# An AdaLN block on one core: loads and first norms in another order, keys kept in pairs of blocks, 640-column scores cut at 384

## The chip, the core and the metric

The kernel runs on one core of a Trainium2 chip. Times are device microseconds (us) of one execution. Three timed executions gave 2437.5, 2437.94 and 2440.83 us; the median, 2437.94 us, is the time before. The profile is of another execution, which took 2422.97 us. The engines are TensorE (PE, with its weight loads as PEld), VectorE (DVE), ScalarE (ACT), GpSimd (POOL) and SyncE (SP), which here only issues transfers.

## What is computed

All data is float32. One token block of 2048 rows and 512 columns goes through an attention layer and a mixture-of-experts layer, each behind a layer norm that is scaled and shifted by a modulation row. Cut to what the change touches, the reference is:

```python
mod = (_silu(L0_c) @ L0_wmod).reshape(1, 6, 1, -1)      # six rows of 512
sa, ca, ga, sb, cb, gb = (mod[:, i] for i in range(6))
h = _layernorm(x, axis=-1) * (1 + ca) + sa
q = jnp.einsum('bpm,hmd->bphd', h, Q_w) + Q_b           # 16 heads of 128; k and v alike
logits = jnp.einsum('bqhd,bkhd->bhqk', q, k) / math.sqrt(128)
scores = softmax(where(key > query, NEG, logits))        # causal, over 2048 keys
attn = jnp.einsum('bhqk,bkhd->bqhd', scores, v)
x = x + ga * (jnp.einsum('bqhd,hdm->bqm', attn, O_w) + O_b)
# then a second norm with sb, cb, and 64 routed experts and 2 shared ones, scaled by gb
```

## The kernel before

The work runs in three stages: a prologue (up to 54.4 us in the profile), the attention over 16 heads (to 1667 us), and the output projection's rest with the experts (to the end). Only the first two are touched.

**Prologue.** SP issues the loads in the order of the code: `c` (L264), then for each of four blocks of 512 tokens the block `xb` of x (L269, 1 MB). After block 0 it issues the two modulation weights `wm` for rows 1 (`ca`) and 0 (`sa`) (L277, 1 MB each), after block 1 the weights of head 0 (L150, L151) and three biases (L286), and after block 3 the weights of the next heads. `mod_row(i)` (L309, L314) makes one modulation row on PE and copies it out with DVE; `mod_turn(i)` (L319, L327) turns it into columns `modT`. `norm_x(b)` (L333 to L339) takes the statistics of a block on DVE, a square root on ACT (L336), a reciprocal (L337), and normalises the block in place with four instructions (L339). `turn_x` (L351) transposes a half of the normalised block on PE into one of two PSUM tiles; `place_x` (L360, ACT) scales and shifts it by `modT` into `hT` and frees the PSUM tile. `plain` (L168, L175) makes the keys and queries of head 0. The order of the calls, written out in the code, is the order on every engine: each engine works through its own instructions in that order.

**Attention.** The work is cut into 80 steps, 5 for each head. Step s of a head handles one or two pairs of 128-row query tiles: pairs 7, 6, (5, 0), (4, 1), (3, 2). `softmax_tile` takes a query tile's causal width in chunks of up to 1024 keys. For each chunk, PE makes the scores in products of up to 512 columns (L500), DVE adds the causal mask on the last 128 columns (L512), takes the row maximum (L513, L517), and ACT makes the exponentials (L519), which frees the PSUM tile `ps`; there are two such tiles, of 1024 columns each. Widths are multiples of 128; a chunk of 640 columns is a product of 512 and one of 128. There are two such chunks in a head (query tiles 4 and 12), 32 in all. Blocks of the finished probabilities are swapped by DMA (L544), turned by DVE (L554), and multiplied with the values on PE (L572).

The scores run two steps ahead of the values. `merge` interleaves the scores, the value products and "fillers" by their share of columns done. The fillers of steps 0 to 2 make queries and keys of the next head: `project(hd + 1, 1)` for tokens 1024 to 2047, then `project(hd + 1, 0)` for tokens 0 to 1023, each of seven parts `first` to `seventh` with a product of their own (L217). The third part writes the keys of the lower block of 512 of its two with one DVE instruction (L235), the fourth those of the upper one (L243). Step 1 of head `hd` ends with the third part of `project(hd + 1, 0)`; in the same step, running two ahead, stand the scores of step 3 of head `hd`, among them the second chunk of query tile 8 (1152 keys: 1024 and 128).

**Keys.** `ktp` is a pool of six tiles of 512 keys each. A head uses four. A new tile is given when one is free, and a tile is free when its last reader is done. Of the keys 1024 to 2047 of a head, the upper tile (1536 to 2047) is read for the last time in step 1 of the head, the lower one (1024 to 1535) in step 3, by that 128-column product.

The lines that follow are the functions that the change touches, with the line numbers of the profile before.

Of the kernel before, what the change touches and what calls it, by code (L numbers as in the profile page):

```python
# [9 lines left out]
F32 = mybir.dt.float32  # L10
# [8 lines left out]
P = 128  # L19
# [4 lines left out]
def adaln_block_kernel(  # L24
# [23 lines left out]
    nc = tc.nc  # L48
    _, N, D = x.shape
    H, _, DH = Q_w.shape  # L50
    E, _, HE = Wg.shape
    S, _, HS = Sg.shape
# [3 lines left out]
    DC = D // P  # L56
# [4 lines left out]
    SC = 1024  # L61
# [59 lines left out]
    with ExitStack() as att:  # L121
        enter = att.enter_context
# [10 lines left out]
        qkb = acst.tile([P, 4, H], F32)  # L133

        qkw = enter(tc.tile_pool(name="qkw", bufs=1))
        ktp = enter(tc.tile_pool(name="ktp", bufs=6))
        qtp = enter(tc.tile_pool(name="qtp", bufs=6))
        heads = {}
        groups = {}
        kts = {}  # L140
        qts = {}
        vts = {}

        def load_head(hd):
            if hd == 0:
                wq, wk = [ktp.tile([P, DC, DH], F32, name="kt") for _ in range(2)]
            else:
                wq = qkw.tile([P, DC, DH], F32, name="wq")
                wk = qkw.tile([P, DC, DH], F32, name="wk")
            nc.sync.dma_start(out=wq, in_=Q_w[hd].rearrange("(k p) d -> p k d", p=P))  # L150
            nc.sync.dma_start(out=wk, in_=K_w[hd].rearrange("(k p) d -> p k d", p=P))  # L151
            return wq, wk
# [10 lines left out]
        def plain(b, j, dst):  # L163
# [12 lines left out]
                dst, ps, AF.Identity, bias=qkb[:, b, 0:1], scale=scale if b == 0 else 1.0  # L176
            )

        def first_tiles():
            for j in (2, 3, 0, 1):  # L180
                kts[0, j] = ktp.tile([P, 512], F32, name="kt")
            for j in (3, 2, 1, 0):
                qts[0, j] = qtp.tile([P, 512], F32, name="qt")

# [22 lines left out]
        def project(hd, b):  # L207


            i, j = 2 * b, 2 * b + 1  # L210
            T = Ts[b]
            box = {}

            def product(l, r):
                ps = psA.tile([P, 512], F32, name="pqk", tag="mm")
                for k in range(2):
                    nc.tensor.matmul(  # L217
                        out=ps, lhsT=l[:, k], rhs=r[:, k], start=(k == 0), stop=(k == 1)
                    )
                return ps  # L220

            def first():
                box["p"] = qkw.tile([P, 512], F32, name="p_")
                ps = product(heads[hd][0][:, 0:2, :], hTs[i][:, 0:2, :])
                nc.scalar.activation(
                    box["p"], ps, AF.Identity, bias=qkb[:, 0, hd : hd + 1], scale=1.0
                )

            def second():
                q = qts[hd, j] = qtp.tile([P, 512], F32, name="qt")  # L230
                nc.vector.tensor_add(q, box["p"], product(sums_w[hd][:, 1], T[:, 1]))

            def third():
                k = kts[hd, i] = ktp.tile([P, 512], F32, name="kt")
                nc.vector.scalar_tensor_tensor(  # L235
                    k, product(sums_w[hd][:, 2], T[:, 2]), qkb[:, 3, hd : hd + 1], qts[hd, j],
                    ALU.add, ALU.add,
                )

            def fourth():  # L240
                k = kts[hd, j] = ktp.tile([P, 512], F32, name="kt")
                ps = product(sums_w[hd][:, 0], T[:, 0])
                nc.vector.tensor_add(k, kts[hd, i], ps)  # L243
                nc.vector.tensor_add(qts[hd, j], qts[hd, j], ps)

            def fifth():
                k = kts[hd, i]
                nc.vector.tensor_sub(k, k, product(heads[hd][1][:, 2:4, :], T[:, 3]))

            def sixth():  # L250
                q = qts[hd, j]
                nc.vector.tensor_add(q, q, product(sums_w[hd][:, 3], hTs[j][:, 2:4, :]))

            def seventh():
                q = qts[hd, i] = qtp.tile([P, 512], F32, name="qt")
                nc.vector.tensor_add(
                    q, box["p"], product(heads[hd][0][:, 2:4, :], hTs[i][:, 2:4, :])
                )

            return [(1024, f) for f in (first, second, third, fourth, fifth, sixth, seventh)]  # L260

        with tc.tile_pool(name="pre", bufs=1) as pre, tc.manual_schedule():
            c4 = pre.tile([DC, P], F32)
            nc.sync.dma_start(out=c4, in_=c.rearrange("o (k p) -> (o k) p", p=P))  # L264
            xs = []
            b16s = []
            for b in range(NB):
                xb = pre.tile([P, 4, D], F32, name="xb", bufs=NB)
                nc.sync.dma_start(  # L269
                    out=xb, in_=x[0, b * 512 : (b + 1) * 512, :].rearrange("(i p) d -> p i d", p=P)  # L270
                )
                xs.append(xb)
                if b == 0:
                    wms = {}
                    for i in (1, 0):
                        wms[i] = pre.tile([P, DC, D], F32, name="wm", bufs=2)
                        nc.sync.dma_start(  # L277
                            out=wms[i],
                            in_=wmod[:, i * D : (i + 1) * D].rearrange("(k p) n -> p k n", p=P),
                        )  # L280
                if b == 1:
                    heads[0] = load_head(0)
                    first_tiles()
                    for src in (Q_b, K_b, V_b):
                        b16 = pre.tile([H, DH], F32, name="b16", bufs=3)
                        nc.sync.dma_start(out=b16, in_=src)  # L286
                        b16s.append(b16)
            groups[0] = load_group(0)
            heads[1] = load_head(1)
            groups[1] = load_group(1)  # L290
# [38 lines left out]
            def norm_x(b):  # L329
                mv = pre.tile([P, 4, 2], F32, name="mv", bufs=2)  # L330
                for i in range(4):
                    st = pre.tile([P, 6], F32, name="st", bufs=4)
                    nc.vector.bn_stats(st, xs[b][:, i, :])  # L333
                    nc.vector.bn_aggr(mv[:, i, :], st)
                rstd = pre.tile([P, 4], F32, name="rstd", bufs=2)
                nc.scalar.activation(rstd, mv[:, :, 1], AF.Sqrt, bias=eps, scale=1.0)  # L336
                nc.vector.reciprocal(rstd, rstd)  # L337
                for i in range(4):
                    nc.vector.tensor_scalar(  # L339
                        xs[b][:, i, :], xs[b][:, i, :], mv[:, i, 0:1], rstd[:, i : i + 1],  # L340
                        ALU.subtract, ALU.mult,
                    )

            turns = {}

            def turn_x(b, half):
                tp = psA.tile([P, 2, 512], F32, name="tp", tag="sc")
                for j in range(2):
                    k = 2 * half + j
                    for i in range(4):  # L350
                        nc.tensor.transpose(  # L351
                            tp[:, j, i * P : (i + 1) * P], xs[b][:, i, k * P : (k + 1) * P], ident
                        )
                turns[b, half] = tp
# [7 lines left out]
                        scale=mod[1][:, k : k + 1], bias=mod[0][:, k : k + 1],  # L362
                    )

            norm_x(0)
            mod_row(1)
            turn_x(0, 0)
            mod_turn(1)
            mod_row(0)
            turn_x(0, 1)  # L370
            mod_turn(0)
            place_x(0, 0)
            place_x(0, 1)
            norm_x(1)
            bps = psA.tile([P, 3, H], F32, name="bps", tag="po")
            for b in range(3):
                nc.tensor.transpose(bps[:, b], b16s[b], ident[:H, :H])
# [5 lines left out]
            for b in range(1, NB):  # L383
                for half in range(2):
                    turn_x(b, half)
                    place_x(b, half)
                if b + 1 < NB:
                    norm_x(b + 1)
                if b == 2:
                    sum_h(0)  # L390
                plain(1, b - 1, kts[0, b - 1])
# [17 lines left out]
        for g in range(1, NG):  # L409
            o = vplace[g - 1]  # L410
# [46 lines left out]
        def softmax_tile(hd, s, pr, i, pb):  # L457
# [35 lines left out]
            def chunk(n):  # L493
                c0 = n * SC
                w = min(SC, width - c0)
                q = qts[hd, qi // 4][:, (qi % 4) * P : (qi % 4 + 1) * P]
                ps = psA.tile([P, SC], F32, name="ps", tag="sc")
                for o in range(0, w, 512):
                    wo = min(512, w - o)
                    nc.tensor.matmul(  # L500
                        out=ps[:, o : o + wo],
                        lhsT=q,
                        rhs=kts[hd, (c0 + o) // 512][:, :wo],
                        start=True,
                        stop=True,
                    )
                if n == 0:
                    box["nm"] = smp.tile([P, 2], F32, name="nm")
                    box["sums"] = smp.tile([P, 2], F32, name="sums")
# [161 lines left out]
        xts = {}  # L671

        def load_x_tile(t):
            if t < 2:
                xts[t] = ktp.tile([P, 512], F32, name="kt")
            else:
                xts[t] = qtp.tile([P, 512], F32, name="qt")
            nc.sync.dma_start(out=xts[t], in_=x[0, t * P : (t + 1) * P, :])

# [806 lines left out]
```

## Time and profile before

| what | value |
|---|---|
| median of three timed executions | 2437.94 us |
| profiled execution, whole | 2422.97 us |
| its span, first to last instruction | 2421.2 us |
| prologue, 0 to 54.4 us | PE busy 39.34 us |
| start of attention, 54.4 to 113 us | PE busy 52.88 of 58.60 us |
| attention, 113 to 1667 us | PE busy 1532.04 of 1554.00 us |
| experts, 1667 to 2421 us | PE busy 738.28 of 754.00 us |
| mean granted TensorE clock | 0.996 |

Every product in float32 is two records of PE in the trace, each behind a weight load of its own, which overlaps the product before it. In a timeline row, the first number is the start in us from the span's start, the second the length of the merged stretch; "x4" is four records, and what stands in brackets is the idle time of that engine just before and what ended it. In a row of groups, the numbers behind the bar are busy us and mean ns of one record.

### The profile page before, as it was taken

To read this page: it belongs to the slowest core of one execution; us is meant where nothing else is said; L and a number is where in the kernel's file an instruction comes from. 1 tells how busy PE (TensorE), PEld (TensorE's weight loads), DVE (VectorE), ACT (ScalarE), POOL (GpSimd) and SP (SyncE) were. 2 spreads that over 40 slices of the span, in tenths; PEclk is the share of its full clock that TensorE was granted. 3 is DMA by queue.
4 is the path that set the end of the run, shared out by engine and by line. 5 is a ranking of instruction groups with operands and counts; after the bars stand their busy time and mean duration, and the time that the engine had idled before them with its cause. 6 is when DMAs were issued, how large, how long until landed. Compare 5 with 4: busy or idle time off the path is not lost. (4 is left out here: it accounts for less than half of the span.)

```text
span 2421.2 us, 26178 instructions
## 1 busy us (share of the span) xinstructions
PE 2362.5 (98%) x8406; PEld 1500.5 (62%) x8406; DVE 1513.2 (62%) x2878; ACT 829.8 (34%) x1737; POOL 219.2 (9%) x286
## 2 busy tenths in 40 slices
PE   7999999999999999999999999999999999999999
PEld 3566656666566665666656656555444476877743
DVE  5367666676676767767666666774655563654564
ACT  3243443444444444444444443432211221222200
POOL 0000000000000000000000000000000111111074
PEclk9999999999999999999999999999999999999999
DMA  4224444454454444444435445564432368877665
GB/s 139 64 71 116 120 118 109 98 143 102 101 127 105 117 120 96 114 111 103 112 93 129 110 99 120 164 194 134 152 122 87 98 203 246 236 217 240 191 194 158
DMA packets 223681, 325.22 MB, mean 134 GB/s; under 512 B 31876, under 2 KB 138424, under 8 KB 223544
## 3 DMA queue, kind: packets, MB, share of 16 engines
q1 hardware_dynamic: 196664, 252.21, 40.3%
q0 software_dynamic: 17664, 54.54, 7.5%
q10 hardware_dynamic: 9216, 16.78, 1.8%
q8 instruction: 68, 1.11, 0.2%
q14 instruction: 69, 0.57, 0.1%
HBM read 138.86 MB, written 41.94 MB: 75 GB/s over the span
## 5 line engine op out<-in xcount | busy, mean ns | idle before, releaser
L519 ACT ACTIVATE p<-ps,nm 128x1024 f32<-128x1024 f32 (+7 forms) x384 | 332.4, 866 | 885.1 <-DVE nm L517 403.9
L572 PEld LDWEIGHTS po<-pt,v 128*128 128x128 f32 x2304 | 426.5, 190 | 249.8 <-issue 187.8
L572 PE MATMUL po<-pt,v 128*128 128x256 f32 (+1 forms) x2304 | 572.3, 368 | 6.6 <-DVE pt L554 5.2
L500 PE MATMUL ps<-kt,qt 128*128 128x512 f32 (+3 forms) x1280 | 531.2, 531 | 20.9 <-ACT p L519 18.7
L513 DVE TENSOR_REDUCE nm<-ps 128x1 f32<-128x1024 f32 (+7 forms) x384 | 348.9, 909 | 48.9 <-PE ps L500 40.2
L554 DVE STREAM_TRANSPOSE pt<-pt 128x1664 f32<-128x1664 f32 (+2 forms) x160 | 318.0, 1988 | 56.3 <-DMA pt<-p 51.4
L500 PEld LDWEIGHTS ps<-kt,qt 128*128 128x128 f32 x1280 | 234.7, 190 | 180.9 <-issue 137.0
L427 PE MATMUL pv<-wv,hT 128*128 128x256 f32 x1024 | 240.8, 379 | 2.2 <-ACT v L434 2.2
L586 POOL DMA_DIRECT2D atd<-at x128 | 74.4, 584 | 1617.4 <-ACT at L581 1155.8
L427 PEld LDWEIGHTS pv<-wv,hT 128*128 128x128 f32 x1024 | 194.4, 190 | 31.2 <-ACT v L434 3.0
L714 ACT ACTIVATE p<-p,rs 128x1024 f32<-128x1024 f32 (+7 forms) x256 | 200.5, 807 | 6.2 <-DVE rs L475 5.9
L1056 PE MATMUL pso<-hT,T 128*128 128x512 f32 x384 | 174.8, 600 | 0.0
L217 PE MATMUL pqk<-T,sw 128*128 128x512 f32 x360 | 169.2, 592 | 0.0
L512 DVE TENSOR_TENSOR ps<-ps,causal 128x128 f32<-128x128 f32 x256 | 74.3, 290 | 150.0 <-PE ps L500 147.6
L1348 PE MATMUL pse<-wgu,xbT 128*128 128x256 f32 x512 | 121.1, 379 | 0.0
L1056 PEld LDWEIGHTS pso<-hT,T 128*128 128x128 f32 x384 | 70.1, 192 | 72.1 <-issue 71.3
L217 PE MATMUL pqk<-hT,wq 128*128 128x512 f32 x240 | 114.1, 598 | 0.0
L1265 PE MATMUL psd<-wsd,hs 128*128 128x512 f32 x256 | 111.5, 592 | 0.0
L1348 PEld LDWEIGHTS pse<-wgu,xbT 128*128 128x128 f32 x512 | 93.8, 190 | 11.7 <-issue 1.0
L217 PEld LDWEIGHTS pqk<-T,sw 128*128 128x128 f32 x360 | 68.3, 190 | 47.8 <-issue 43.0
L1331 POOL DMA_INDIRECT xb<-h2d,tok x64 | 65.2, 1018 | 301.8 <-PE tpx L1341 275.1
L1343 ACT COPY xbT<-tpx 128x512 f32<-128x512 f32 x64 | 37.4, 586 | 146.0 <-DVE y L1371 54.4
(365 smaller groups left out, 2344.3 us busy)
## 6 DMA issues: line engine op xcount, KB each, us to landing
pt<-p SPq DMA_DIRECT2D x768, 104.0 KB, 2.2
pt<-p SPq DMA_DIRECT2D x256, 124.0 KB, 2.3
pt<-p SPq DMA_DIRECT2D x256, 108.0 KB, 2.2
atd<-at POOLq DMA_DIRECT2D x128, 128.0 KB, 2.2
wgu<-in_L_ffn_Wg_dram SPq DMA_DIRECT2D x64, 256.0 KB, 4.6
wgu<-in_L_ffn_Wu_dram SPq DMA_DIRECT2D x64, 256.0 KB, 4.9
wd<-in_L_ffn_Wd_dram SPq DMA_DIRECT2D x64, 256.0 KB, 3.7
ybd<-y ACTq DMA_DIRECT2D x64, 256.0 KB, 3.8
```

What stands on the lines that cost most here:

```text
L217: nc.tensor.matmul(out=ps, lhsT=l[:, k], rhs=r[:, k], start=(k == 0), stop=(k == 1))
L427: nc.tensor.matmul(out=ps, lhsT=hTs[t // 4][:, k, (t % 4) * P : (t % 4 + 1) * P], rhs=wv[:, k].rearrange("p i d -> p (i d)"), start=(k == ...
L500: nc.tensor.matmul(out=ps[:, o : o + wo], lhsT=q, rhs=kts[hd, (c0 + o) // 512][:, :wo], start=True, stop=True,)
L513: nc.vector.tensor_reduce(nm[:, n : n + 1], ps[:, :w], AX.X, ALU.max, negate=True)
L519: nc.scalar.activation(rows[:, r0 + c0 // P : r0 + (c0 + w) // P], ps[:, :w].rearrange("q (r b k) -> q r b k", b=4, k=32), AF.Exp, bias=nm ...
L554: nc.vector.transpose(part, part)
L572: nc.tensor.matmul(out=po if wide else po[:, P:], lhsT=vts[g, kt // 4][:, kt % 4, hh * DH : (hh + 1) * DH], rhs=rows[:, r : r + last + 1 : ...
L586: nc.gpsimd.dma_start(out=atd[hd, :, o * 256 : (o + 1) * 256], in_=at[:, m])
L714: nc.scalar.activation(part, part, AF.Identity, scale=r)
L1056: nc.tensor.matmul(out=ps, lhsT=abs_[pr][:, hd, i * P : (i + 1) * P], rhs=wos[hd // 4][:, hd % 4, :], start=(hd == 0), stop=(hd == H - 1),)
L1265: nc.tensor.matmul(out=ps, lhsT=hsh[b, f][:, i * P : (i + 1) * P], rhs=wsd[:, f, :], start=(f == 0), stop=(f == NHC - 1),)
L1348: nc.tensor.matmul(out=ps, lhsT=xts[e][:, k, :], rhs=weights[e][:, k].rearrange("p i h -> p (i h)"), start=(k == 0), stop=(k == DC - 1),)
```

## The change

Five edits:

1. The weights `wm` of modulation row 1 are loaded ahead of block 0 of x, those of row 0 behind it, then blocks 1 to 3; the weights of head 0 and the biases follow block 3 instead of block 1.
2. `norm_x` becomes a generator that stops after the reciprocal and after the normalisation. For block 1, the statistics, the root and the reciprocal now stand behind `turn_x(0, 1)` and ahead of `mod_turn(0)`, and the normalisation stands behind `mod_turn(0)` and ahead of `place_x(0, ...)`. On DVE this puts the `modT` of row 0 behind the reciprocal of block 1.
3. `ktp` holds three tiles of two blocks of 512 keys in place of six of one. The third part of `project` takes a whole pair, and the fourth writes into its other half. Head 0's weights, and two of the x tiles loaded near the end, take a pair too.
4. The scores read a pair as 1024 columns, which any cut may cross at 512.
5. A chunk of 640 columns starts at column 128 of its PSUM tile and is cut into products of 384 and 256 columns, so that each stays in one half of the tile; other chunks are cut at 512 as before.

```diff
-        ktp = enter(tc.tile_pool(name="ktp", bufs=6))
+        ktp = enter(tc.tile_pool(name="ktp", bufs=3))
...
+        def key_tiles(hd, b):
+            kps[hd, b] = ktp.tile([P, 2, 512], F32, name="kt")
+            for i in range(2):
+                kts[hd, 2 * b + i] = kps[hd, b][:, i]
+
         def first_tiles():
-            for j in (2, 3, 0, 1):
-                kts[0, j] = ktp.tile([P, 512], F32, name="kt")
+            for b in (1, 0):
+                key_tiles(0, b)
...
             def third():
-                k = kts[hd, i] = ktp.tile([P, 512], F32, name="kt")
+                key_tiles(hd, b)
+                k = kts[hd, i]
...
             def fourth():
-                k = kts[hd, j] = ktp.tile([P, 512], F32, name="kt")
+                k = kts[hd, j]
...
+            load_wm(1)
             for b in range(NB):
                 xb = pre.tile([P, 4, D], F32, name="xb", bufs=NB)
...
                 if b == 0:
...
+                    load_wm(0)
+            heads[0] = load_head(0)
+            first_tiles()
+            for src in (Q_b, K_b, V_b):
+                b16 = pre.tile([H, DH], F32, name="b16", bufs=3)
+                nc.sync.dma_start(out=b16, in_=src)
+                b16s.append(b16)
...
                 nc.vector.reciprocal(rstd, rstd)
+                yield
                 for i in range(4):
...
+                yield
...
-            norm_x(0)
+            for _ in norm_x(0):
+                pass
             mod_row(1)
             turn_x(0, 0)
             mod_turn(1)
             mod_row(0)
             turn_x(0, 1)
+            scale_x = norm_x(1)
+            next(scale_x)
             mod_turn(0)
+            next(scale_x)
             place_x(0, 0)
             place_x(0, 1)
-            norm_x(1)
...
-                for o in range(0, w, 512):
-                    wo = min(512, w - o)
-                    nc.tensor.matmul(
-                        out=ps[:, o : o + wo],
-                        lhsT=q,
-                        rhs=kts[hd, (c0 + o) // 512][:, :wo],
-                        start=True,
-                        stop=True,
-                    )
+                keys = kps[hd, c0 // SC].rearrange("p j n -> p (j n)")
+                if w == 640:
+                    ps = ps[:, P : P + w]
+                    cuts = (0, 384, 640)
+                else:
+                    cuts = (0, min(w, 512), w)
+                for a, b in zip(cuts, cuts[1:]):
+                    if a < b:
+                        nc.tensor.matmul(
+                            out=ps[:, a:b], lhsT=q, rhs=keys[:, a:b], start=True, stop=True
+                        )
```

More of the change, by code (lines that the diff above doesn't have):

```diff
@@ L140, in adaln_block_kernel @@
         kts = {}
+        kps = {}
         qts = {}
@@ L145, in load_head @@
             if hd == 0:
-                wq, wk = [ktp.tile([P, DC, DH], F32, name="kt") for _ in range(2)]
+                both = ktp.tile([P, 2, 512], F32, name="kt")
+                wq, wk = [both[:, i].rearrange("p (k d) -> p k d", k=DC) for i in range(2)]
             else:
@@ L264, in adaln_block_kernel, with load_wm @@
             nc.sync.dma_start(out=c4, in_=c.rearrange("o (k p) -> (o k) p", p=P))
+            wms = {}
+            def load_wm(i):
+                wms[i] = pre.tile([P, DC, D], F32, name="wm", bufs=2)
+                nc.sync.dma_start(
+                    out=wms[i],
+                    in_=wmod[:, i * D : (i + 1) * D].rearrange("(k p) n -> p k n", p=P),
+                )
             xs = []
             b16s = []
+            load_wm(1)
             for b in range(NB):
@@ L273, in adaln_block_kernel @@
                 if b == 0:
[L274 to L279, printed above, removed]
-                        )
[L281 to L287, printed above, removed]
+                    load_wm(0)
[5 more added lines that the diff above has]
+                b16s.append(b16)
             groups[0] = load_group(0)
@@ L387, in adaln_block_kernel @@
                 if b + 1 < NB:
-                    norm_x(b + 1)
+                    for _ in norm_x(b + 1):
+                        pass
                 if b == 2:
@@ L497, in chunk @@
                 ps = psA.tile([P, SC], F32, name="ps", tag="sc")
-                for o in range(0, w, 512):
-                    wo = min(512, w - o)
-                    nc.tensor.matmul(
-                        out=ps[:, o : o + wo],
-                        lhsT=q,
-                        rhs=kts[hd, (c0 + o) // 512][:, :wo],
-                        start=True,
-                        stop=True,
-                    )
+                keys = kps[hd, c0 // SC].rearrange("p j n -> p (j n)")
[8 more added lines that the diff above has]
+                            out=ps[:, a:b], lhsT=q, rhs=keys[:, a:b], start=True, stop=True
+                        )
                 if n == 0:
@@ L673, in load_x_tile @@
         def load_x_tile(t):
-            if t < 2:
-                xts[t] = ktp.tile([P, 512], F32, name="kt")
-            else:
+            if t == 0:
+                both = ktp.tile([P, 2, 512], F32, name="kt")
+                xts[0], xts[1] = both[:, 0], both[:, 1]
+            if t >= 2:
                 xts[t] = qtp.tile([P, 512], F32, name="qt")
```

## The prediction

> **What bounds the kernel now.** I read the page's busy shares first, then busy times by stage (the table above), then the costliest groups, then the timeline of one head.
>
> ```profile
> span 2421.2 us, 26178 instructions
> PE 2362.5 (98%) x8406; PEld 1500.5 (62%) x8406; DVE 1513.2 (62%) x2878; ACT 829.8 (34%) x1737; POOL 219.2 (9%) x286
> L500 PE MATMUL ps<-kt,qt 128*128 128x512 f32 (+3 forms) x1280 | 531.2, 531 | 20.9 <-ACT p L519 18.7
> ```
>
> PE is busy 98% of the span, so a change counts by what it does to PE: columns to stream, or time in which PE stands still. The third row says where PE stands still in the attention: 18.7 us ahead of the score products, until ACT has emptied a `ps` tile. Heads 1 to 15 repeat every 98 to 102 us, and each has two such stops. The long one (1.01 us at 332.06) lies in step 0; the short one, 0.11 us of PE's own idle time, lies in step 1. The short one of head 2's projection, in the timeline of all engines:
>
> ```profile
> 250.38 1.90 DVE L554 STREAM_TRANSPOSE pt<-pt 128x1664 f32<-128x1664 f32 x1
> ...
> 252.28 0.75 DVE L235 SCALAR_TENSOR_TENSOR kt<-pqk,qkb,qt 128x512 f32<-128x512 f32 x1
> ...
> 252.51 1.03 PE L500 MATMUL ps<-kt,qt 128*128 128x128 f32 x4
> 252.95 0.29 DVE L512 TENSOR_TENSOR ps<-ps,causal 128x128 f32<-128x128 f32 x1
> ...
> 253.28 0.29 DVE L513 TENSOR_REDUCE nm<-ps 128x1 f32<-128x128 f32 x1
> ...
> 253.60 0.16 DVE L517 TENSOR_TENSOR nm<-nm 128x1 f32<-128x1 f32 x1
> ...
> 253.80 0.37 ACT L519 ACTIVATE p<-ps,nm 128x128 f32<-128x128 f32 x1 [3.16 <-DVE nm L517]
> ...
> 254.31 0.30 PEld L500 LDWEIGHTS ps<-kt,qt 128*128 128x128 f32 x2 [0.30 <-ACT p L519]
> 254.31 1.12 PE L500 MATMUL ps<-kt,qt 128*128 128x512 f32 x2
> ```
>
> See how tight it is: DVE goes from a turn of probabilities straight to the key write L235 (`third`), straight to the mask L512, to the maximum; ACT makes the exponential; PE has already run dry and starts the next scores 0.14 us after the exponential ends. Any delay of L235 lands on PE in full.
>
> **The new wait (edit 3).** With six single tiles, `third` of `project(hd + 1, 0)` takes the tile of keys 1536 to 2047, free since early in step 1. With three pairs, the free one is the pair 1024 to 2047, and its last reader is the 128-column product of query tile 8, which stands *behind* `third`'s own product on PE, one value product later. The two programs as built say the same: in 15 heads (1 to 15), L235 waits for this product where it waited for its own; apart from the mask behind it, which no longer needs that wait, and waits that name the last product of a 640 chunk, no wait between PE, DVE and ACT changes in the attention. Queued behind L235 on DVE are the mask and maximum of that very chunk; ACT's exponential waits for them, and PE's next scores for ACT.
>
> Price: the row at 252.51 merges two products, 128 and 384 columns. Two records of 128 columns start 0.11 us apart, and the group of that shape has a mean of 274 ns, so the first product ends at 252.62 + 0.27 = 252.89. DVE starts some 0.04 us after a product's end (elsewhere: end 320.93, start 320.97). So L235 moves from 252.28 to 252.93, by 0.65 us, and PE's start at 254.31 by as much, since PE already waits there. In the same view 13 heads have L235 start 0.23 us ahead of that product, as here; head 1 gives 0.57 us and head 8, where DVE is later, 0.38 us. Sum: 13 x 0.65 + 0.57 + 0.38 = **9.4 us**. Bounds for one: 0.38 and 0.75 us, the smallest seen and one whole L235. Nothing downstream takes it back: the long stop in the next step 0 hangs on a chain that PE's own 384-column product starts at 329.37, and moves along.
>
> **The cut (edits 4 and 5).** Starts of neighbouring rows give the price of a product, from PE's timeline:
>
> ```profile
> 103.06 1.24 PE L500 MATMUL ps<-kt,qt 128*128 128x512 f32 x4
> 104.14 3.60 PE L168 MATMUL pqk<-hT,kt 128*128 128x512 f32 x8
> ...
> 132.52 0.81 PE L500 MATMUL ps<-kt,qt 128*128 128x384 f32 x2
> 133.16 0.59 PE L572 MATMUL po<-pt,v 128*128 128x256 f32 x2
> ```
>
> A pair of 512 and 128 columns holds PE from 103.06 to 104.14: 1.08 us. A product of 384 holds it 0.64 us, one of 256 (142.62 to 143.05) 0.43 us: 1.07 us. The trace gives 1.079 against 1.077 by single records, so 32 chunks save 0.1 us. A rule speaks for more: the Trainium skill's "TensorE: Matmul & The Clock Gate", section "Back-to-back issue gap", gives about 81 ns for a matmul of 128 columns with its weight load, against 56 ns alone. Taken for both records of 32 products, that would be an estimate of 2 x 32 x 25 ns = 1.6 us saved. The rows show float32 records of 128 columns 109 ns apart, a quarter of the 429 ns of 512 columns, with the weight loads hidden. The row decides: **-0.1 us**; the -1.6 stays for the range. DVE and ACT read as many columns as before, and neither stop of PE is at a 640 chunk.
>
> **The prologue (edits 1 and 2).** From 31.6 us PE runs nearly without a break, so the price is the shift of that point.
>
> Loads: block 0 lands at 6.9 us and `wm` of row 1 at 9.7 (DVE and PE start on them then). They change places, 2.8 us each. `norm_x(0)` took 6.88 to 12.66 and now ends at 15.4. `mod_row(1)` starts at 6.9, takes 5.85 us, and has to wait: its row copy stands behind that norm on DVE and runs 15.4 to 16.1. `mod_turn(1)` takes 1.05 us, so `mod_row(0)` starts at about 17.25, against 17.48. The early start has bought 0.2 us, and PE is left with 8 transposes and 8 tiny products between 12.75 and 17.25. Does its clock hold?
>
> ```profile
> 21.09:24.50 3.41, 2.19 (x19) 1.92 (x19) 2.03 (x5) 1.18 (x2) 0.00 (x0) 1.00 1.19 302
> 24.50:27.91 3.41, 0.20 (x1) 0.18 (x1) 2.90 (x9) 1.90 (x4) 0.00 (x0) 0.50 0.75 177
> 27.91:31.33 3.42, 3.42 (x14) 2.67 (x14) 3.35 (x12) 0.93 (x2) 0.00 (x0) 0.50 0.00 0
> ```
>
> These are busy times by window (length, PE, PEld, DVE, ACT, POOL, then the granted clock). PE was busy 2.19 of 3.41 us, with the same mix of transposes and tiny products, and the next window was granted half. The same page of the skill, Part 1, says that it takes at least one idle window of about 3.4 us to fall to half; the longest idle stretch here is 1.3 us (12.75 to 14.05), so by the rule `mod_row(0)` keeps its 3.59 us. By the row it spends a window at half speed: 4 of 8 records at 0.855 us in place of 0.43 (both spacings are in the first `mod_row`), 5.3 us.
>
> By the row: row copy at 22.5 to 23.2; then, new on DVE ahead of `modT`, block 1's statistics to reciprocal (23.20 to 27.03 before, 3.83 us), `modT` at 27.2 instead of 23.12; `place_x(0)` 27.3 to 30.1 instead of 23.32 to 26.11; block 1 normalised 27.2 to 29.1 instead of 27.06 to 28.98. PE's first transposes of block 1 now wait also for a PSUM tile, until 28.7, but ACT's `place_x(1)` ends at 33.5 against 33.26, the root of block 2 follows at once, and everything after is 0.3 us late. By the rule all of this is 1.7 us earlier: -1.4 us. I take the row, **+0.3 us**, and keep -1.4.
>
> Other moves on SP: the biases come behind 2 MB more of x, land at about 22.8 us in place of 17.4, and are wanted at 24.3 by PE (L377), ahead of transposes that cannot start before 28.7. Head 0's weights land about then and are wanted at 31.6. Blocks 2 and 3 only come earlier. All hidden; if the biases were late by more than 4 us, PE would pay the excess. The x tiles near the end take a pair already free: nothing.
>
> **Sum.** 9.4 - 0.1 + 0.3 = +9.6 us. The profiled execution would go from 2422.97 to 2432.6 us. The timed ones lie 15 us above it with nothing in the trace to say why; I carry the difference over: 2437.94 + 9.6 = **2447.5 us**.
>
> **Rivals.**
> - *The prologue pays the wait back* (not slower). PE stands still from 23.2 to 27.7 us and then transposes at half clock, 4.5 + 1.3 us (13 transposes in 2.50 us against 1.40 at 35.66). If block 1's early statistics closed the gap, up to 5.8 us would go. From 4.5 us on, the sum falls under the 0.2% line: 9.3 - 4.6 gives 2442.6. Against it: `modT` of row 0 now waits for those statistics, and ACT's placing with it.
> - *The wait costs nothing*: the pool hands `third` another pair, or PE finds other work. Then -0.1 and 0.3: 2438.1. Against it: the built program's wait, and 15 stops of PE behind that chain already.
> - *The prologue also loses*: all of `mod_row(0)` at half clock (8 x 0.43 = 3.4 us more than 3.59, 1.7 more than in my sum): 2449.2.
> - *Clock and cut as the rules have it*: -1.4 and -1.6: 9.4 - 3.0 gives 2444.3.
>
> **How the numbers follow.** 0.2% is 4.9 us, about what a measurement tells from no change. Chances: my forecast 0.60, rules 0.12, prologue loses 0.12 (all slower, 0.84); paid back 0.07 and no cost 0.05 (same, 0.12); anything under 2433.1, for which no part of the sum gives a reason, 0.04. The range reaches down past the rules to where the prologue pays most of it back, and up past the third rival by what 15 waits of 0.75 us would add (1.9 us): 2441.5 to 2451.
>
> **What would show it.** Right: in 15 heads, L235's successor idle some 0.6 us until the PE product of `ps`; PE's short stops grown from 0.11 to about 0.75 us, and the idle ahead of the score products from 18.7 to about 28 us; 640 chunks at 1.08 us as before; first scores at 54.4 to 55 us. Wrong: short stops of 0.1 us as before, or first scores ahead of 52 us.

## The result and the profile after

Over 20 timed executions of each kernel the median went from 2436.65 to 2447.34 us: a ratio of 1.0039, 95% interval 1.0032 to 1.0047. The changed kernel is slower by 10.7 us; the forecast was 9.6 us more, 2447.5 us. Its profiled execution took 2449.41 us, 26.4 us more than that of before. The page of after, its span, its busy shares and its group of score products (L500 is now L523):

```profile
span 2447.6 us, 26179 instructions
PE 2372.1 (97%) x8406; PEld 1510.3 (62%) x8406; DVE 1512.5 (62%) x2878; ACT 828.3 (34%) x1737; POOL 218.7 (9%) x286
L523 PE MATMUL ps<-kt,qt 128*128 128x512 f32 (+3 forms) x1280 | 531.6, 531 | 31.2 <-ACT p L538 30.4
```

The products are as many and as long as before (531.6 against 531.2 us). What grew is the last column, PE's idle time ahead of the scores: 20.9 to 31.2 us. The view of waits of this line in the attention (113 to 1697 us), its part on who waited for a score product (us, times), has a row that the view of before had not:

```profile
  DVE kt L243: 9.7, 15
```

L243 is the key write of `third` (L235 before). It waits 15 times, 0.65 us in 14 heads and 0.50 us in head 1. The all-engine timeline of after at the place of head 2 that the prediction showed (start us, length, engine and line; idle time and releaser in brackets):

```profile
257.31 1.91 DVE L573 STREAM_TRANSPOSE pt<-pt 128x1664 f32<-128x1664 f32 x1
...
259.44 1.03 PE L523 MATMUL ps<-kt,qt 128*128 128x128 f32 x4
...
259.87 0.75 DVE L243 SCALAR_TENSOR_TENSOR kt<-pqk,qkb,qt 128x512 f32<-128x512 f32 x1 [0.65 <-PE ps L523]
...
260.53 0.29 DVE L531 TENSOR_TENSOR ps<-ps,causal 128x128 f32<-128x128 f32 x1
...
261.38 0.37 ACT L538 ACTIVATE p<-ps,nm 128x128 f32<-128x128 f32 x1 [3.82 <-DVE nm L536]
...
261.88 0.70 PE L523 MATMUL ps<-kt,qt 128*128 128x512 f32 x1 [0.76 <-ACT p L538]
```

The turn ends at 259.22 as tight as before; then DVE stands 0.65 us until the 128-column product is done, and mask, maximum, exponential and PE follow late: PE's stop is 0.76 us where it was 0.11. Over all heads these short stops (idle time of under 0.9 us ahead of a score product that follows a value product, 16 in each kernel, the last of them some 0.4 us near the end of the attention in both) sum to 2.35 us before and 11.79 us after.

The 26 us between the two profiled executions come apart by landmarks:

| where | before | after | difference, us |
|---|---|---|---|
| first scores | 54.38 | 56.95 | +2.6 |
| 16 short stops | 2.35 in all | 11.79 in all | +9.4 |
| half clock from some 114 us on | 3.4 long | 6.8 long | +1.0 |
| head 2, step 0 (a DMA late for DVE, then a window at half clock) | stop of 1.54 | stop of 2.63 | +2.8 |
| a stop of PE near the end, after's with half clock behind it | 1.16 | 10.63 | +11.7 |

The rows sum to 27.5 us; small differences elsewhere take 1 us back. The last row is no work of the change; the runs below place it.

### The profile page after: what moved, and what is told of

Its sections match the earlier page's. It is cut to its first block, busy times and chain, and to the rows that moved or that the text cites. A ratio compares the mean times of both kernels' runs of the same rounds, so it can differ in the third digit from the quotient of the medians.

```text
span 2447.6 us, 26179 instructions
## 1 busy us (share of the span) xinstructions
PE 2372.1 (97%) x8406; PEld 1510.3 (62%) x8406; DVE 1512.5 (62%) x2878; ACT 828.3 (34%) x1737; POOL 218.7 (9%) x286
## 5 line engine op out<-in xcount | busy, mean ns | idle before, releaser
L523 PE MATMUL ps<-kt,qt 128*128 128x512 f32 (+3 forms) x1280 | 531.6, 531 | 31.2 <-ACT p L538 30.4
L523 PEld LDWEIGHTS ps<-kt,qt 128*128 128x128 f32 x1280 | 234.7, 190 | 184.3 <-issue 121.7
L444 PEld LDWEIGHTS pv<-wv,hT 128*128 128x128 f32 x1024 | 194.4, 190 | 31.2 <-ACT v L451 3.0
L224 PE MATMUL pqk<-T,sw 128*128 128x512 f32 x360 | 169.2, 592 | 0.0
L224 PE MATMUL pqk<-hT,wq 128*128 128x512 f32 x240 | 114.5, 600 | 0.0
L1368 PEld LDWEIGHTS pse<-wgu,xbT 128*128 128x128 f32 x512 | 93.8, 190 | 11.7 <-issue 1.0
L224 PEld LDWEIGHTS pqk<-T,sw 128*128 128x128 f32 x360 | 68.4, 190 | 47.7 <-issue 43.1
L1363 ACT COPY xbT<-tpx 128x512 f32<-128x512 f32 x64 | 37.4, 585 | 146.0 <-DVE y L1391 54.4
```

The source lines that it names most:

```text
L224: nc.tensor.matmul(out=ps, lhsT=l[:, k], rhs=r[:, k], start=(k == 0), stop=(k == 1))
L444: nc.tensor.matmul(out=ps, lhsT=hTs[t // 4][:, k, (t % 4) * P : (t % 4 + 1) * P], rhs=wv[:, k].rearrange("p i d -> p (i d)"), start=(k == ...
L523: nc.tensor.matmul(out=ps[:, a:b], lhsT=q, rhs=keys[:, a:b], start=True, stop=True)
L1368: nc.tensor.matmul(out=ps, lhsT=xts[e][:, k, :], rhs=weights[e][:, k].rearrange("p i h -> p (i h)"), start=(k == 0), stop=(k == DC - 1),)
```

## The experiments

Times are medians; "before" in a row is the kernel before, timed alongside on the same chip. It stood at 2439.19 and 2437.65 us in two series on one chip and at 2425.67 us in one series on another, so only ratios are compared across series. "Stops" is the sum of the short stops as counted above, "attention" the time from the start of the first score product to that of the last product of the output projection (L688 of before); these two and the first scores are from one profiled execution of each run.

| run | edits | us | before | ratio (95%) | first scores | stops | attention |
|---|---|---|---|---|---|---|---|
| before again | none, one execution | 2439.09 | | | 55.29 | 2.3 | 1630.1 |
| pairs and cut | 3 to 5 | 2447.51 | 2439.19 | 1.0032 (1.0020 to 1.0044) | 54.51 | 11.84 | 1642.7 |
| prologue alone | 1, 2 | 2439.23 | 2439.19 | 1.0000 (0.9991 to 1.0009) | 55.26 | 2.06 | 1630.8 |
| third behind | all, `third` later | 2430.96 | 2439.19 | 0.9965 (0.9951 to 0.9979) | 55.10 | 0.4 | 1623.9 |
| late fillers | none, `third` later still | 2415.91 | 2425.67 | 0.9958 (0.9944 to 0.9971) | 54.12 | 0.41 | 1619.0 |
| pairs late | 3 to 5, `third` later still | 2416.07 | 2425.67 | 0.9957 (0.9943 to 0.9970) | 54.84 | 0.40 | 1619.1 |
| loads alone | 1 | 2438.56 | 2437.65 | 1.0006 (0.9996 to 1.0015) | 56.28 | 2.14 | 1628.6 |
| norms alone | 2 | 2435.87 | 2437.65 | 0.9994 (0.9987 to 1.0002) | 53.56 | 2.33 | 1631.9 |
| warm prologue | all, and three products more | 2436.72 | 2425.67 | 1.0048 (1.0033 to 1.0063) | 54.14 | 11.83 | 1638.6 |
| early statistics | none of the change | 2411.43 | 2425.67 | 0.9941 (0.9928 to 0.9955) | 51.81 | 0.39 | 1619.3 |
| late turn | none of the change | 2417.32 | 2437.65 | 0.9922 (0.9908 to 0.9935) | 49.16 | 0.4 | 1614.2 |

**The halves of the change.** First the attention's edits on the prologue of before, then the prologue's edits on the attention of before. Each run has one half of the diff of the change and nothing of the other; cut to its first lines:

```diff
 pairs_and_cut
-        ktp = enter(tc.tile_pool(name="ktp", bufs=6))
+        ktp = enter(tc.tile_pool(name="ktp", bufs=3))
...
 prologue_alone
+            load_wm(1)
...
+            scale_x = norm_x(1)
+            next(scale_x)
             mod_turn(0)
+            next(scale_x)
```

> Edits 3 to 5 alone, with the prologue of before. Theory (the new wait of third on the key pair): each of heads 1 to 15 has PE's short stop ahead of the scores grown from 0.11 to about 0.76 us, first scores at 54.4 us as before, and the time some 9 us (0.37%) over before. Rival (the pairs cost nothing, the prologue is what slows the changed kernel): short stops of 0.11 us and the time within 2 us of before.

> Edits 1 and 2 alone, with six single key tiles and cuts at 512. Theory: short stops of 0.11 us as before; first scores 0 to 3 us later than 54.4 us, because mod_row(0) runs at half clock for part of its length; the time 0 to 4 us over before. Rival (the wait is nothing, the prologue all of it): the time 9 us or more over before.

The attention's half alone costs 8.3 us (1.0032), which its interval doesn't tell from the 10.7 us of the whole change, and it has the stops of after (11.84 us); the prologue's half alone costs nothing that 13 executions can tell (1.0000, within 0.1%), and its stops are those of before. The rival in which the prologue pays the wait back, and the one in which the wait costs nothing, are out.

**Is it the wait itself?** The pair could also cost something else: another place in memory, another cut. This run keeps the whole change and moves the third part, its product on PE included, behind the 128-column product in PE's order, so that the pair is free when it is asked for. The weights by which the interleaving places the fillers of step 1 are changed:

```diff
                 n = 4 if s == 2 else 5
                 out = ahead[:n]
                 del ahead[:n]
+                if s == 1:
+                    out = [(c, f) for c, (_, f) in zip((1100, 1100, 1100, 1100, 720), out)]
                 return out
```

> The changed kernel with third moved behind the 128-column product that it has to wait for, and nothing else: the weights of the fillers of step 1 in the interleaving are 1100 x 4 and 720 in place of 1024 x 5. Theory: DVE's key write finds its pair free, the mask no longer stands behind it, and the short stops vanish or stay under 0.15 us: 9 to 15 us less than the changed kernel, so about 0 to -4 us against before with the prologue's 2.6 us in it. Rival (the pair's release is not what holds DVE, the key write itself is): short stops of 0.7 us stay and the time is that of the changed kernel.

The all-engine timeline of this run at the same place of head 2:

```profile
252.28 0.38 PE L523 MATMUL ps<-kt,qt 128*128 128x128 f32 x2
...
252.50 1.88 PE L224 MATMUL pqk<-T,sw 128*128 128x512 f32 x4
...
254.42 0.75 DVE L243 SCALAR_TENSOR_TENSOR kt<-pqk,qkb,qt 128x512 f32<-128x512 f32 x1
254.51 0.37 ACT L538 ACTIVATE p<-ps,nm 128x128 f32<-128x128 f32 x1 [2.40 <-DVE nm L536]
...
255.52 1.88 PE L523 MATMUL ps<-kt,qt 128*128 128x512 f32 x4
```

Now the 128-column product stands ahead of `third`'s (L224), L243 waits for nothing and comes behind the chunk's mask and maximum, and the last row has no bracket: PE doesn't stop. The short stops are gone, but for one of 0.41 us that before has too, and the kernel is 8.2 us faster than before, 16.5 us faster than pairs and cut. More than the 9.4 us of the new wait went, since the stop of before went too. The key write on DVE had hardly held that one: in 13 of 15 heads of before the mask starts only 0.05 us after the end of its 128-column product (0.10 and 0.29 us in heads 1 and 8), and DVE starts some 0.04 us after a product's end in any case. What went is PE's lack of work: the product of `third`, 1.7 us, now runs behind the 128-column product while DVE and ACT work on the chunk. So this run changes two things, the wait for the pair and the place of that product; the two runs of the next part tell them apart. From the start of one product to the start of the next, the 16 stops of before again cost 5.0 us, some 0.16 us each more than PE's idle time of 2.3 us shows, and other score products lost 3.3 us where 1.8 are left here; these two make 6.0 us of the 6.2 that the attention is shorter (1630.1 to 1623.9). The long stops of step 0 stayed (15, 18.35 us).

**The long stops.** The same move, `third` still later, on the kernel before, in steps 0 and 1, and once more with the pairs and the cut:

```diff
+                if s < 2 and out:
+                    out = [(c, f) for c, (_, f) in zip((1240, 1240, 1240, 1240, 160), out)]
```

> The kernel before, with only the weights of the fillers of steps 0 and 1 changed to 1240 x 4 and 160, so that the fifth part of project(hd + 1, 1) and the third of project(hd + 1, 0), 1.7 us of PE each, stand behind the last score product of their step. Theory (both stops are PE running dry behind the chain mask, maximum, exponential, and a filler there covers them): the short stops of 0.11 us and the long ones of 1.0 us or more vanish; with the 0.28 and 0.1 us of each restart that is about 0.4 and 1.3 us in 15 heads, 25 us less than before. Rival (the stops move with the fillers to another place of the step): 10 us or less saved, and new stops of PE in the attention in their place.

> Edits 3 to 5 with the prologue of before and the same late fillers. Theory: with third behind the last reader of its pair the pairs cost nothing, and the cuts at 384 save 0.1 us: the same time as the late fillers on the kernel before, within 1.5 us. Rival (products of 128 columns pay for a weight load that is not hidden[...]): 2 us or more less than the late fillers alone. Rival (a second cost of the pairs is left): 2 us or more over them.

Both came out alike, 2415.91 and 2416.07 us, attention 1619.0 and 1619.1 us: **with `third` behind its tile's last reader, pairs cost nothing and the cut gains nothing** that these runs can tell. That settles the cause: with `third` ahead of the reader the same pairs and cut made the attention 12.6 us longer (1630.1 to 1642.7), with `third` behind it 0.1 us. But 9.8 us were saved where the theory had 25: the short stops went, the long ones didn't. All idle time ahead of the scores went from 21.0 us (before again) to 14.0 us. The timeline of the first of the two shows why the long stop of step 0 shrank (from 1.01 us) without going away:

```profile
326.85 0.81 PE L500 MATMUL ps<-kt,qt 128*128 128x384 f32 x2
...
327.38 1.97 DVE L554 STREAM_TRANSPOSE pt<-pt 128x1728 f32<-128x1728 f32 x1
...
329.28 0.27 DVE L512 TENSOR_TENSOR ps<-ps,causal 128x128 f32<-128x128 f32 x1
...
331.09 1.98 PE L500 MATMUL ps<-kt,qt 128*128 128x512 f32 x4 [0.84 <-ACT p L519]
```

The score products stand earlier in the step now. The one at 326.85 is done at 327.66, but its mask starts at 329.28: DVE's turn of probabilities (1.97 us) is ahead of it. In before the same product ended at 330.18 (329.37 and 0.81) and its mask began at 330.22, the turn being over by then. So PE, which now has a filler to do, still waits 0.84 us at the next score product. Behind the one wait stood another.

**The prologue.** Loads alone and norms alone, the two edits taken apart, then the whole change with three products more. They are 512 columns long, stand in the gap around the first transposes, and nobody reads their results:

```diff
+            def keep_busy(n):
+                hot = psA.tile([P, 512], F32, name="hot", tag="mm")
+                for i in range(n):
+                    nc.tensor.matmul(
+                        out=hot[0:1, :], lhsT=sg[:, 0:1], rhs=wms[1][:, i % DC, :],
+                        start=True, stop=True,
+                    )
...
             mod_row(1)
+            keep_busy(2)
             turn_x(0, 0)
+            keep_busy(1)
             mod_turn(1)
```

> Edit 1 alone: the order of the loads. Theory (the loads swap which of mod_row(1) and norm_x(0) is first, leave PE lightly used behind mod_row(1), and halve the clock of mod_row(0)): the second mod_row takes over 5 us in place of 3.59; with modT of row 0 still ahead of block 1's statistics, first scores at 55 to 57 us. Rival (the loads do no harm, the order on DVE does): the second mod_row at 3.6 us, first scores at 54 to 55.3 us.

> Edit 2 alone: statistics of block 1 behind turn_x(0, 1), modT of row 0 behind its reciprocal, normalisation behind that; loads as before. Theory: the second mod_row stays at 3.59 us; modT of row 0 comes 2.2 us later than in before but block 1 is normalised 1.6 us earlier against its own copy of row 0; first scores 1 to 2 us earlier than in before (54.4 to 55.3), at 52.5 to 54 us. Rival (the late modT costs as much as the early statistics give): 54.4 us or later.

> The changed kernel with three more products of 512 columns on PE whose results nobody reads, two behind mod_row(1) and one behind the first transposes, 0.86 us each at full clock, in the time in which PE waits for DVE. Theory (mod_row(0) was slow because PE's light use between 12.7 and 18.3 us halved its clock): the second mod_row takes 3.6 us in place of 5.5, and first scores come at 53.5 to 55 us in place of 56.9. Rival (only a whole idle window drops the clock, and the profiled execution was an accident of phase): the second mod_row takes 3.6 us here and in the other executions of the same prologue without the extra products; or it stays at 5 us with them.

PE's timeline of after in the prologue, and the busy times by window of its second row to the end of its fourth (columns as in the prediction, granted clock third from the right):

```profile
6.40 6.30 PE L320 MATMUL pmr<-wm,sg 128*1 128x512 f32 x8 [3.93 <-DMA wm<-in_L_wmod_dram]
13.89 2.70 PE L364 MATMUL tp<-ident,xb 128*128 128x128 f32 x8 [1.19 <-DVE xb L351]
16.52 1.86 PE L330 MATMUL pmt<-ones,row 1*128 1x1 f32 x8
18.31 5.47 PE L320 MATMUL pmr<-wm,sg 128*1 128x512 f32 x8
```

```profile
12.70:18.31 5.61, 4.04 (x17) 3.13 (x17) 2.69 (x7) 0.30 (x1) 0.00 (x0) 0.73 1.05 387
18.31:23.78 5.47, 5.47 (x10) 0.83 (x10) 0.16 (x1) 0.00 (x0) 0.00 (x0) 0.65 1.17 306
```

And the same of the warm prologue:

```profile
14.43 1.53 PE L364 MATMUL tp<-ident,xb 128*128 128x128 f32 x8
15.89 1.02 PE L381 MATMUL hot<-wm,sg 128*1 128x512 f32 x2
16.84 1.05 PE L330 MATMUL pmt<-ones,row 1*128 1x1 f32 x8
17.82 3.59 PE L320 MATMUL pmr<-wm,sg 128*1 128x512 f32 x8
```

```profile
12.70:17.82 5.12, 4.99 (x23) 2.09 (x22) 2.68 (x6) 0.28 (x1) 0.00 (x0) 1.00 1.05 386
```

Eight transposes, eight tiny products and the second `mod_row`: 2.70, 1.86 and 5.47 us in after, 1.53, 1.05 and 3.59 us with three long products among them. Loads alone gave 5.29 us for that `mod_row`, norms alone 3.60: it is the early load of `wm` that spreads PE's little work thin and loses the clock. The first scores of the 2 x 2, averaged over the profiled executions there are: neither edit 54.6 us (54.12 to 55.29, five executions: both profiles of before, pairs and cut, late fillers, pairs late), loads 56.3 and norms 53.6 (one each), both 55.8 (55.10 to 56.95, three). Both together are some 1.1 us late, but the scatter of one cell is as large, and the timed ratios (1.0006, 0.9994, 1.0000) tell none of it from nothing. Warm or not, the ratio of the whole kernel stays above 1 (1.0048, on the other chip): the prologue is not where the change loses.

**A version that beats both.** Two steps on, from the kernel before: the statistics of block 1 moved further up, and then DVE's second turn of step 0 moved past the mask.

```diff
             mod_turn(1)
+            scale_x = norm_x(1)
+            next(scale_x)
             mod_row(0)
             turn_x(0, 1)
             mod_turn(0)
+            next(scale_x)
...
-                    marks.append((0.8, lambda: turn(n + 1, 1)))
+                    marks.append((0.97 if s == 0 else 0.8, lambda: turn(n + 1, 1)))
```

Both keep the late fillers; `norm_x` stops in two places as in edit 2, and `norm_x(1)` behind `place_x` is left out. The last line is in the second alone.

> The kernel before with the late fillers, and its prologue with one move: the statistics, root and reciprocal of block 1 stand behind mod_turn(1) and ahead of mod_row(0), where DVE was idle from 17.8 to 21.1 us, and its normalisation behind mod_turn(0). Loads as before. Theory: modT of row 0 comes at about 23.7 us as before, block 1 is normalised by 25.6 in place of 29.0, PE's gap ahead of its transposes shrinks from 4.5 to about 2 us, first scores at 50 to 52 us in place of 54.4 to 55.3: 3 us less than the late fillers alone. Rival (PE's clock falls all the same and takes it back): first scores at 53.5 us or later.

> The late fillers and early statistics, with the second turn of probabilities of step 0 (L554, 2.0 us of DVE) moved from 0.8 to 0.97 of the step, behind the masks and maxima. Theory (what is left of the long stop, 0.84 us at 331.09 with the late fillers, is DVE turning probabilities from 327.38 to 329.35 while the finished 384-column product waits for its mask): the stop vanishes, with its restart about 1.1 us in 15 heads, 16 us less than late fillers with early statistics. Rival (the turn then holds back the first value product of the next step, which needs both halves): a new stop of PE ahead of the value products, and no more than 5 us saved.

The first brings 4.5 us over late fillers on the same chip (2411.43 against 2415.91); first scores at 51.81 in place of 54.12 are 2.3 us of it in the profiled executions, and where the rest lies is not shown. The second is 20.3 us under before (0.9922), but its gain in the attention is 5 us (1614.2 against 1619.3), as its rival had it, not the 16 us of the stops that it removes. Groups of PE lines in the attention of that run:

```profile
L578 PE MATMUL po<-pt,v 128*128 128x256 f32 (+1 forms) x2244 | 554.2, 368 | 10.3 <-DVE pt L560 10.3
L506 PE MATMUL ps<-kt,qt 128*128 128x512 f32 x1244 | 513.0, 528 | 0.4 <-ACT p L525 0.4
```

PE no longer waits ahead of the scores (0.4 us in all), but now the value products wait for the turn that was put back, L560: 10.3 us. The first scores at 49.16 us, 2.7 us ahead of the run before it on the other chip, are nothing that this edit touches. Their traces differ in the clock: late turn was granted full clock from 24.00 to 31.00 us, early statistics half clock from 23.90 to 30.73 us, and the first eight records of `plain` (L168) behind the transposes took 3.60 us against 4.92. What a prologue gives can thus differ by over 2 us between two single executions.

## Why the prediction was right, step by step

- **The new wait, +9.4 us.** Right in place, mechanism and size: 15 waits of 0.65 us on L243, short stops from 0.11 to 0.76 us, 9.4 us in sum. That the wait was the cause is shown by the pairs with `third` ahead of their last reader and behind it: 12.6 us of the attention against 0.1. (Single executions scatter: with the fillers as in before the attention took 1628.6 to 1631.9 us in five with single tiles, 1638.6 to 1642.7 in three with pairs.) That nothing downstream takes it back held too: of these 12.6 us 9.5 lie in the short stops and 1.9 in the long ones. Heads 1 and 8, which the forecast set apart at 0.57 and 0.38 us, waited 0.50 and 0.65. All idle time ahead of the scores grew by 10.3 us (20.9 to 31.2) where 9.4 was forecast; head 2's step 0 (1.1 us) is the largest known part of the rest.
- **The cut, -0.1 us.** Right by the row: a 640 chunk takes 1.077 us in all 32 cases, 1.079 before. On PE's timeline of after, in head 2, the start of one chunk and of what follows it:

```profile
278.11 1.24 PE L523 MATMUL ps<-kt,qt 128*128 128x384 f32 x4
279.19 1.04 PE L591 MATMUL po<-pt,v 128*128 128x128 f32 x6
```

  The 1.6 us estimated from the Trainium skill's figure for a short matmul weren't there; pairs late and late fillers differ by 0.16 us.
- **The prologue, +0.3 us.** The choice was right, the size too small. `mod_row(0)` lost its clock as the row of before foretold (5.3 to 5.5 us in four executions), and not by the rule in the table of the Trainium skill's "TensorE: Matmul & The Clock Gate", Part 1, that takes an idle window for it. But the term counted one window, from `mod_row(0)` on. In the profiled execution of after half the clock was granted earlier (0.50 from 15.29 us on), so that the transposes and tiny products ahead of it stretched too (2.70 and 1.86 us), and `mod_row(0)` started at 18.31, not 17.25. First scores came some 1.1 us late on the average of three executions, 2.6 us in the profiled one, in place of 0.3, at 55.1 to 56.95 us where 54.4 to 55 was forecast. The third rival named a loss of about this size, but put all of it into `mod_row(0)`; it adds to the forecast and doesn't change its sign.
- **The 15 us carried over** between profiled and timed executions was an unknown, and that carrying it was right is luck as much as judgement. It is for the most part the stop near the end: PE's timeline of before, and then the all-engine timeline of before again, the same kernel:

```profile
2364.84 3.70 PE L1119 MATMUL psg<-h2T,wsu 128*128 128x512 f32 x8 [1.16 <-DVE sig L1108]
```

```profile
2357.32 0.69 DVE L1272 TENSOR_TENSOR acc<-acc,psd 128x512 f32<-128x512 f32 x1 [13.90 <-remote]
...
2364.70 3.78 PE L1119 MATMUL psg<-h2T,wsu 128*128 128x512 f32 x4 [10.56 <-DVE sig L1108]
```

  Before again took 2439.09 us in this execution, like the median, and has the stop; the profiled execution of before (2422.97) hasn't. After's has it (10.63 us). 2422.97 us lies under all timed executions of before on the first chip (2433.09 us and up) and 0.9 us under the lowest on the second (2423.89); on which chip that profile was taken is not on record. Without that stop, the pair of profiles differs by some 15 us: 9.4 are the wait, 2.6 the prologue, 2.8 head 2's step 0 and 1.0 the half clock behind the prologue; the last two were not in the forecast.
- **The sum.** 9.6 us forecast, 10.7 measured, with an interval of 7.8 to 11.5 us: the total is right, but it is too coarse to confirm the terms one by one. The traces do that for the wait and the cut; they show the prologue's term too small.

## What to carry to other kernels

A coarser buffer pool is shorter to write, but it moves the moment at which either half comes free to the later of the two halves' last readers; before merging tiles, find the last reader of each half in the program order and see whether the new writer stands ahead of it. If it does, move the writer behind the reader: that cost two lines here and turned a loss of 0.4% into a gain of 0.35%, more than the loss, because the writer's own product, moved along with it, gave PE work at a place where it had run dry before as well. And when a stop is removed, read what stands next in the queues of the in-order engines: here the late place of the score products hid a turn of probabilities ahead of their mask, and that turn's place hid the wait of the value products for it, so that of 21 us of idle time ahead of the scores 14 were still there when the fillers had moved, and putting the turn back, which ended these 14, gave only 5.

## What the runs showed of the hardware

- **A stop of 10 to 16 us near the end that went with the chip, not with the kernel.** Of seven profiled executions on one chip six have it (9.8 to 16.4 us of PE; the seventh has 4.6 and 2.6 us in its place); the four on another haven't (0.8 to 2.2 us), over kernels that do the same work there; and before's median differs between the two by 12 to 14 us (2439.19 and 2437.65 against 2425.67). In it DVE waits 13.9 us for something the profile calls only "remote", while POOL's indirect gathers run; ACT and PE wait for DVE. What holds it stays open: no run took it apart, and the second chip served in one series only.
- **Half clock without an idle window.** In after the stretch from 12.70 to 18.31 us had PE busy for 4.04 of 5.61 us and a mean clock of 0.73, and the 5.47 us behind it got 0.65. Three 512-column products in the gap (4.99 of 5.12 us busy) kept it at 1.00. Busy time made of transposes of 128 columns and products of one column didn't hold the clock here. It need not lose it either: in late turn PE was busy 2.49 of 4.00 us from 20.00 to 24.00 us, mostly with such work, and the 7.00 us behind it got 1.00. So the busy share alone doesn't decide; what does, the runs don't tell.
